# First keys in four pieces, weight inspections four to a slot, and token rows split behind a slot's values, in a two-layer gated cross-attention kernel

## The chip, the core and the metric

The kernel runs on one core of a Trainium2 chip. A core has five engines that run their own instruction queues in order and wait for each other by semaphores: TensorE (PE in the profile; its weight loads are PEld), VectorE (DVE), ScalarE (ACT), GpSimd (POOL), and SyncE (SP), which here only issues transfers. Work lies in SBUF (128 partitions) and matrix products are summed in PSUM, in banks of 128 x 512 f32. The metric is the device time of one execution in microseconds (us), the median of several runs.

## The reference

Eight images (B = 8) of 100 query tokens x of width 512 each attend to 722 context tokens of their own, twice, and after each attention there is a feed-forward stage on the 800 tokens. What is computed:

```
x = x + tanh(g_xattn[0]) * attention0(layernorm(x), ctx, ctx, mask)      # 16 heads of 32
x = x + tanh(g_ffn[0])   * ffn0(layernorm(x))
x = x + tanh(g_xattn[1]) * attention1(layernorm(x), ctx, ctx)            # with an output projection
x = x + tanh(g_ffn[1])   * ffn1(layernorm(x))

ffn0: h = silu(x W1 * s1) * (x W2 * s2);  h = gelu(h H1 * t1);  h = gelu(h H2 * t2);  y = h W3 * s3
      # 512 -> 2048 -> 2048 -> 2048 -> 512, weights of ffn0 are -1, 0 or 1, with a scale for each output
ffn1: the same gated form with weights and activations rounded to few levels first
```

The change lies in attention0: its keys, its slots, and what is done beside them for ffn0.

## The kernel before, in words

**Stages.** Attention 0 takes the first 590 us or so, ffn0 follows in two halves of 400 tokens, then attention 1 and ffn1. There is no planner: the order of every engine's instructions is written out by the program's own order, with generators that are advanced at fixed places (`next(...)`, `yield`). `take(us)` advances the generator in `state["fill"]`, the TensorE work that fills gaps, by about so many us.

**Start.** SyncE issues the loads in this order: key bias, key weights `wk` (1 MB), the first 384 context tokens of image 0 (`load_ctx(0, 0)`, 768 KB), value weights `wv`, the first four images' tokens x, query weights, the rest of the context, the other tokens, and small things. `projections` makes keys `kT` (`make`, L313 to 351): for each of four output chunks `oc`, four products over the input chunks `c` are summed in one bank of the pool `ps_p` (two banks), and ScalarE copies the sum out with the bias. Then the values of the same context tokens, L334 to 349. Queries follow (`queries`, L355), fed by normalised rows (`ln_turned`, L167): VectorE computes `ln_v`, GpSimd the root by a power (`ln_root`, L150), VectorE refines it (`ln_rstd`, L153 to 162) and scales rows (`ln_apply`, L165), TensorE turns them.

**Slots.** `attention` (L389) runs over 8 images b and 4 groups oc of four heads: 32 slots. In a slot TensorE makes the scores of a group in two halves (four banks of `ps_sc`), VectorE adds the mask, takes maxima and writes the rows `p` (L410), and ScalarE takes exponents (L427). Between the halves and behind them the next image's keys and values are made. Then `between(b, oc)` is called, and `settle` (L512) finishes the slot before: six times TensorE turns a block of `p` into one of the two banks of `ps_t` (L442), ScalarE or VectorE copies it out (L447, L445), and `values` (L450) sums the products with v in a free part of the fifth block's bank; VectorE copies that out (L461). At an image's end `finish` (L463) normalises, adds to x and takes the row statistics.

**Beside the slots.** `inspections` (L711) looks at ffn0's weights before they are used: 88 blocks of 128 x 1024 f32 are fetched by GpSimd's own transfers (two buffers), the low halves of the words are added up by GpSimd (L733, L734), and at the end VectorE takes the maximum (L737), TensorE turns it, and VectorE writes a verdict of 0 or 1. With 0 the products of ffn0 in a short format are exact and nothing more is run; otherwise the whole is computed again in full f32 (not the case with these inputs). `between0` advances the inspections three times a slot:

```
    def between0(b, oc):
        nonlocal entering
        for _ in range(3):
            next(inspected, None)
        ...
        if (b, oc) == (B - 2, KC - 1):
            later["wv"] = weights(a["L1_Wv"], [P, KC, D], "wv1")
            entering = normalised(0, HI_LO[0])
        if (b, oc) >= (B - 2, KC - 1):
            later["xs"] = next(entering)
```

`normalised` (L597) prepares the first 400 tokens for ffn0. Its first step, in slot 27 (b = 6, oc = 3), is the tokens' root, of which GpSimd does the power, and the first image's rows; each further step, in slots 28 to 31, turns one image's rows (L182) into a bank of `ps_t`, and `split` (L588) writes a high part `xa` by ScalarE (L590) and a low part `xc` by VectorE (L591), chunk by chunk; VectorE makes the next image's rows. ffn0's first product is ready to run behind slot 31. Its weight blocks are loaded through GpSimd's queue (`block`, L583).

Of the kernel before, what the change touches and what calls it, by code (L numbers as in the profile page):

```python
# [9 lines left out]
F32 = mybir.dt.float32  # L10
# [16 lines left out]
P = 128  # L27
# [28 lines left out]
def flow(tc: tile.TileContext, a: dict, out: bass.AP, verdict):  # L56
# [30 lines left out]
    def room(shape, name, dtype=F32):  # L87
        return wts.tile(shape, dtype, tag="w", name=name, bufs=3)
# [7 lines left out]
    def weights(src, shape, name):  # L96
        t = room(shape, name)
        nc.sync.dma_start(t, src)
        return t
# [89 lines left out]

    def load_ctx(i, part):  # L190
        k0, kn = PARTS[i // B][part]
        t = rooms["ctx"].tile([P, KC, PARTS[0][0][1]], F32, tag="ctxT", name=f"ctxT{i}_{part}")
        nc.sync.dma_start(t[:, :, :kn], a["ctxT"][i % B][:, :, k0 : k0 + kn])
        ctx_tiles[i, part] = t
# [74 lines left out]
    def projections(i, wk, wv, bk, more):  # L269
# [43 lines left out]
        def make():  # L313
            for part, (k0, kn) in enumerate(PARTS[layer]):
                cT = ctx_tiles.pop((i, part))
                for oc in range(KC):
                    ps = ps_p.tile([P, 512], F32, tag="ps", name="ps_k")
                    for c in range(KC):
                        nc.tensor.matmul(  # L319
                            ps[:, :kn],  # L320
                            wk[:, c, oc * P : (oc + 1) * P],
                            cT[:, c, :kn],
                            start=(c == 0),
                            stop=(c == KC - 1),
                        )
                        if c == KC - 1:
                            nc.scalar.activation(
                                kT[:, oc, k0 : k0 + kn],
                                ps[:, :kn],
                                AF.Identity,  # L330
                                bias=bk[:, oc : oc + 1],
                            )
                        yield kn * MM
                for kc, (r0, rn) in enumerate(KEYS[layer]):  # L334
# [53 lines left out]

    def attention(layer, kv, follow, qT, bias_of, between, wo, bv, bo, pick):  # L389

# [140 lines left out]
        for b in range(B):  # L531
# [11 lines left out]
            for oc in range(KC):  # L543
# [19 lines left out]
                if held is not None:  # L563
                    ending = settle()
                held = (b, oc, v, ps, oT, sums)

        def last():
# [143 lines left out]
    def inspections():  # L711
# [24 lines left out]
        worst = small.tile([P, 1], F32, tag="worst", name="worst")  # L736
        nc.vector.reduce_max(worst, seen, axis=AX.X)  # L737
        pt = ps_t.tile([P, 512], F32, tag="pst", name="ps_seen")
        nc.tensor.transpose(pt[:1, :P], worst, ident)
# [235 lines left out]
    bk = load("L0_bk", [P, KC], "bk0")  # L975
    wk = weights(a["L0_Wk"], [P, KC, D], "wk0")
    load_ctx(0, 0)
    wv = weights(a["L0_Wv"], [P, KC, D], "wv0")
# [74 lines left out]
    def between0(b, oc):  # L1053
        nonlocal entering
        for _ in range(3):
            next(inspected, None)
        if oc == 1 and b + 1 < B:
            state["spare"] = mask_bias(b + 1)
            next(state["spare"])
        if oc == 2:  # L1060
            for _ in state["spare"]:
                pass
        if (b, oc) == (B - 2, KC - 1):
            later["wv"] = weights(a["L1_Wv"], [P, KC, D], "wv1")
            entering = normalised(0, HI_LO[0])
        if (b, oc) >= (B - 2, KC - 1):
            later["xs"] = next(entering)

    ending = attention(0, kv, follow0, qT, lambda b: biases[b], between0, None, bv, None, None)
    for _ in inspected:  # L1070
# [16 lines left out]

    def nothing():
        pass
# [151 lines left out]
    def between1(b, oc):  # L1241
# [26 lines left out]
        lambda b: zero.to_broadcast([S, SK]),  # L1268
        between1,
        wo,  # L1270
        None,
# [107 lines left out]
```

## Time and profile before

| | |
|---|---|
| median of 3 runs | 1755.31 us (1752.71 to 1758.7) |
| the profiled execution's own time | 1753.82 us |
| its span, first to last instruction | 1751.6 us |
| TensorE busy | 1682.2 us (96%) |
| GpSimd busy | 574.1 us (33%) |
| first matmul starts | 8.53 us |
| GpSimd's inspections | 84 of 88 by 414 us, the last four from 506.6 to 522.5 us |
| tokens' root on GpSimd | 505.56 us |
| ffn0's first product | 591.66 us |

How to read the profile: a line of the timeline has the start and the length in us, the engine, the kernel's line, the operation, what it writes and reads, and how many instructions are merged (x4); in brackets stands how long the engine had been idle before it, and what ended that wait. A line of the table of waits has who waited for whom, the total in us, how often, and the longest. Queues of transfers are named after the engine that issues them (SPq, POOLq). Matmul lengths are modelled and overlap; the distance from one start to the next is the surer number.

### The profile page before, as it was taken

To read this page: it belongs to the slowest core of one execution; us is meant where nothing else is said; L and a number is where in the kernel's file an instruction comes from. 1 tells how busy PE (TensorE), PEld (TensorE's weight loads), DVE (VectorE), ACT (ScalarE), POOL (GpSimd) and SP (SyncE) were. 2 spreads that over 40 slices of the span, in tenths; PEclk is the share of its full clock that TensorE was granted. 3 is DMA by queue.
4 is the path that set the end of the run, shared out by engine and by line. 5 is a ranking of instruction groups with operands and counts; after the bars stand their busy time and mean duration, and the time that the engine had idled before them with its cause. 6 is when DMAs were issued, how large, how long until landed. Compare 5 with 4: busy or idle time off the path is not lost.

```text
span 1751.6 us, 30454 instructions
## 1 busy us (share of the span) xinstructions
PE 1682.2 (96%) x12459; PEld 1292.0 (74%) x12459; DVE 848.0 (48%) x2349; ACT 663.6 (38%) x1404; POOL 574.1 (33%) x542
## 2 busy tenths in 40 slices
PE   8999999999988999999999999989999999998887
PEld 4555555555554799999999999868888888885554
DVE  2445466455545430154462110455555576667755
ACT  1143434344334553322232111335445544544442
POOL 0699999993030000000000000133334333310110
PEclk9999999999999999999999999999999999999999
DMA  6345445452030388778685555420001001001000
GB/s 213 121 137 170 148 144 163 148 164 74 25 113 15 121 266 271 256 255 300 206 274 191 168 178 182 152 66 24 24 24 30 24 24 30 24 27 54 10 10 22
DMA packets 63802, 212.31 MB, mean 121 GB/s; under 512 B 7410, under 2 KB 30450, under 8 KB 51294
## 3 DMA queue, kind: packets, MB, share of 16 engines
q0 software_dynamic: 25344, 138.42, 23.8%
q1 hardware_dynamic: 38310, 71.86, 13.5%
q8 instruction: 99, 1.62, 0.4%
q14 instruction: 49, 0.40, 0.1%
HBM read 205.48 MB, written 4.78 MB: 120 GB/s over the span
## 4 chain that ended last, share of the span: by engine, by line
PE 62%; POOL 15%; DVE 8%; issue 8%; DMA 5%; ACT 2%; SPq 0%; DVEq 0%; POOLq 0%; ACTq 0%
PE ps_h L610 27%; POOL seen L734 9%; PE ps_v L259 7%; PE ps_k L259 5%; POOL part L733 4%; PE ps_pT L442 3%; PE sc L401 3%; DMA w_seen<-in_h_w 3%; PE ps_w L688 3%; PE ps_k L319 2%; PE ps_gu L885 2%; PE ps_pT L454 2%; PE ps_q L368 2%; PE ps_wo L497 2%; PE ps_v L339 2%
## 5 line engine op out<-in xcount | busy, mean ns | idle before, releaser
L610 PE MATMUL ps_h<-hi,h 128*128 128x400 f32 x1024 | 355.0, 347 | 0.0
L610 PE MATMUL ps_h<-lo,h 128*128 128x400 f32 x1024 | 354.7, 346 | 0.0
L442 PEld LDWEIGHTS ps_pT<-ident,p 100*128 100x128 f32 (+3 forms) x1536 | 163.4, 138 | 100.4 <-issue 47.3
L427 ACT ACTIVATE p<-p,negm 100x722 f32<-100x722 f32 x256 | 228.1, 894 | 10.8 <-DVE negm L424 10.6
L339 PE MATMUL ps_v<-wv,ctxT 128*128 128x512 f32 (+3 forms) x432 | 215.0, 608 | 0.0
L319 PE MATMUL ps_k<-ctxT,wk 128*128 128x384 f32 (+3 forms) x576 | 204.0, 482 | 8.5 <-DMA ctxT<-in_ctxT 8.5
L442 PE MATMUL ps_pT<-ident,p 100*128 100x100 f32 (+3 forms) x1536 | 196.9, 251 | 15.8 <-DVE pT L445 8.6
L734 POOL TENSOR_TENSOR seen<-seen,part 128x1024 int32<-128x1024 int32 x88 | 209.3, 2379 | 7.5
L591 DVE TENSOR_TENSOR lo<-g,hi 128x400 fp32r<-128x400 f32 x96 | 55.3, 576 | 311.2 <-ACT hi L590 311.2
L610 PEld LDWEIGHTS ps_h<-hi,h 128*128 128x128 f32 x1024 | 192.8, 188 | 0.6
L610 PEld LDWEIGHTS ps_h<-lo,h 128*128 128x128 f32 x1024 | 192.5, 188 | 0.6
L445 DVE COPY pT<-ps_pT 128x400 f32<-128x400 f32 (+1 forms) x180 | 102.5, 570 | 126.3 <-PE ps_pT L442 126.3
L410 DVE CUSTOM_DVE_ANT_0 p<-sc,mask 100x361 f32<-100x361 f32 x256 | 121.2, 530 | 62.7 <-PE sc L401 62.5
L447 ACT COPY pT<-ps_pT 128x400 f32<-128x400 f32 (+2 forms) x204 | 100.0, 492 | 136.1 <-PE ps_pT L442 135.9
L319 PEld LDWEIGHTS ps_k<-ctxT,wk 128*128 128x128 f32 x576 | 101.2, 192 | 67.1 <-issue 30.2
L585 POOL DMA_DIRECT2D h<-in_h_w x64 | 33.9, 529 | 354.7 <-PE ps_h L610 333.5
L663 ACT ACTIVATE g<-ps_h,h_s 128x400 f32<-128x400 f32 x64 | 38.1, 596 | 259.4 <-PE ps_h L610 259.4
L410 DVE CUSTOM_DVE_ANT_0 p<-sc,zero 100x361 f32<-100x361 f32 x256 | 121.7, 530 | 24.1 <-PE sc L401 23.6
L339 PEld LDWEIGHTS ps_v<-wv,ctxT 128*128 128x128 f32 (+3 forms) x432 | 69.5, 185 | 55.0 <-issue 53.4
L213 POOL TENSOR_SCALAR ctx_h<-ctx_raw 128x480 fp32r<-128x480 f32 (+1 forms) x40 | 23.8, 594 | 243.1 <-PE ps_v L259 196.1
L733 POOL CAST part<-w_seen 128x1024 int32<-128x1024 uint16 x88 | 92.7, 1053 | 21.6 <-DMA w_seen<-in_h_w 12.0
L259 PE MATMUL ps_k<-ctx_h,wk_g 128*128 128x240 f32 (+1 forms) x336 | 89.5, 293 | 2.9 <-DVE kT L294 1.7
(205 smaller groups left out, 2912.1 us busy)
## 6 DMA issues: line engine op xcount, KB each, us to landing
h<-in_h_w POOLq DMA_DIRECT2D x64, 1024.0 KB, 5.3
w_seen<-in_h_w POOLq DMA_DIRECT2D x64, 512.0 KB, 4.0
w<-in_w POOLq DMA_DIRECT2D x16, 1024.0 KB, 6.3
w_seen<-in_w POOLq DMA_DIRECT2D x16, 512.0 KB, 4.0
w_gate<-in_w_gate SPq DMA_DIRECT2D x16, 512.0 KB
w_up<-in_w_up SPq DMA_DIRECT2D x16, 512.0 KB
w_down<-in_w_down SPq DMA_DIRECT2D x16, 512.0 KB
w<-in_w_w POOLq DMA_DIRECT2D x8, 1024.0 KB, 7.0
```

What stands on the lines that cost most here:

```text
L259: nc.tensor.matmul(ps[:, col : col + n], w if keys_move else x, x if keys_move else w, start=(c == 0 and k == which[0]), stop=(c == KC - 1 ...
L319: nc.tensor.matmul(ps[:, :kn], wk[:, c, oc * P : (oc + 1) * P], cT[:, c, :kn], start=(c == 0), stop=(c == KC - 1),)
L339: nc.tensor.matmul(ps[:rn, :], cT[:, c, r0 - k0 : r0 - k0 + rn], wv[:, c, :], start=(c == 0), stop=(c == KC - 1),)
L410: nc.vector.tensor_tensor_reduce(ps[j][:, cols], sc[j][:S, :HALF], bias[:, cols], 1.0, LOWEST, ALU.add, ALU.max, m2[:, j, h : h + 1],)
L427: nc.scalar.activation(ps[j], ps[j], AF.Exp, bias=negm[:, j : j + 1], accum_out=sums[:, 4 * oc + j : 4 * oc + j + 1],)
L442: nc.tensor.transpose(pt[:kn, j, :], ps[j][:, k0 : k0 + kn], ident[:S, :S])
L445: nc.vector.tensor_copy(sb[:kn], pt[:kn])
L447: nc.scalar.copy(sb[:kn], pt[:kn])
L591: nc.vector.tensor_sub(two[1][:, cols], src, two[0][:, cols].bitcast(F32))
L610: nc.tensor.matmul(acc[:, :TH], w[:, c, :], part, start=(c == 0 and k == 0), stop=(c == len(ins) - 1 and k == len(two) - 1),)
L733: nc.gpsimd.tensor_copy(part, low)
L734: nc.gpsimd.tensor_tensor(seen, seen, part, ALU.add)
```

## The change

1. `load_ctx(0, 0)` and the load of `wk` become eight transfers: for each input chunk c, the chunk of `wk` and then the chunk of the context. For image 0's first part `make` runs its sixteen products with c outside and oc inside, in four banks of `ps_sc` at once. Everything else in `make` keeps its order.
2. `between0` advances the inspections four times a slot in slots 0 to 21 (88 steps), where it was three in slots 0 to 29.
3. The maximum over the inspection (a new `yield` stands behind it) is taken in slot 29, its transposition and the verdict in slot 30; both were in slot 29.
4. The steps of `normalised` move from `between0`, ahead of `settle`, into `beyond0`, which `attention` calls behind `settle`. Creating the generator and loading the second layer's value weights stay in `between0`. Attention 1 is given a `beyond` that does nothing.

```diff
--- before.py
+++ after.py
@@ -187,10 +187,15 @@
 
     ctx_tiles = {}
 
-    def load_ctx(i, part):
+    def load_ctx(i, part, beside=None):
         k0, kn = PARTS[i // B][part]
         t = rooms["ctx"].tile([P, KC, PARTS[0][0][1]], F32, tag="ctxT", name=f"ctxT{i}_{part}")
-        nc.sync.dma_start(t[:, :, :kn], a["ctxT"][i % B][:, :, k0 : k0 + kn])
+        if beside is None:
+            nc.sync.dma_start(t[:, :, :kn], a["ctxT"][i % B][:, :, k0 : k0 + kn])
+        else:
+            for c in range(KC):
+                nc.sync.dma_start(beside[0][:, c, :], beside[1][:, c, :])
+                nc.sync.dma_start(t[:, c, :kn], a["ctxT"][i % B][:, c, k0 : k0 + kn])
         ctx_tiles[i, part] = t
 
     def split_ctx(i, part, idle=False):
@@ -313,24 +318,32 @@
         def make():
             for part, (k0, kn) in enumerate(PARTS[layer]):
                 cT = ctx_tiles.pop((i, part))
-                for oc in range(KC):
-                    ps = ps_p.tile([P, 512], F32, tag="ps", name="ps_k")
-                    for c in range(KC):
-                        nc.tensor.matmul(
+
+                first = i == 0 and part == 0
+                home, tag = (ps_sc, "sc") if first else (ps_p, "ps")
+                order = [(oc, c) for oc in range(KC) for c in range(KC)]
+                if first:
+                    order.sort(key=lambda t: t[1])
+                sums = {}
+                for oc, c in order:
+                    if c == 0:
+                        sums[oc] = home.tile([P, 512], F32, tag=tag, name="ps_k")
+                    ps = sums[oc]
+                    nc.tensor.matmul(
+                        ps[:, :kn],
+                        wk[:, c, oc * P : (oc + 1) * P],
+                        cT[:, c, :kn],
+                        start=(c == 0),
+                        stop=(c == KC - 1),
+                    )
+                    if c == KC - 1:
+                        nc.scalar.activation(
+                            kT[:, oc, k0 : k0 + kn],
                             ps[:, :kn],
-                            wk[:, c, oc * P : (oc + 1) * P],
-                            cT[:, c, :kn],
-                            start=(c == 0),
-                            stop=(c == KC - 1),
+                            AF.Identity,
+                            bias=bk[:, oc : oc + 1],
                         )
-                        if c == KC - 1:
-                            nc.scalar.activation(
-                                kT[:, oc, k0 : k0 + kn],
-                                ps[:, :kn],
-                                AF.Identity,
-                                bias=bk[:, oc : oc + 1],
-                            )
-                        yield kn * MM
+                    yield kn * MM
                 for kc, (r0, rn) in enumerate(KEYS[layer]):
                     if not k0 <= r0 < k0 + kn:
                         continue
@@ -386,7 +399,7 @@
 
 
 
-    def attention(layer, kv, follow, qT, bias_of, between, wo, bv, bo, pick):
+    def attention(layer, kv, follow, qT, bias_of, between, beyond, wo, bv, bo, pick):
 
         gate = tg[:S, layer : layer + 1]
 
@@ -563,6 +576,7 @@
                 if held is not None:
                     ending = settle()
                 held = (b, oc, v, ps, oT, sums)
+                beyond(b, oc)
 
         def last():
             for _ in exps:
@@ -735,6 +749,7 @@
             yield
         worst = small.tile([P, 1], F32, tag="worst", name="worst")
         nc.vector.reduce_max(worst, seen, axis=AX.X)
+        yield
         pt = ps_t.tile([P, 512], F32, tag="pst", name="ps_seen")
         nc.tensor.transpose(pt[:1, :P], worst, ident)
         most = small.tile([1, 1], F32, tag="most", name="most")
@@ -973,8 +988,8 @@
     rooms["oT"] = pool(right, "oT0", 2, side="right")
 
     bk = load("L0_bk", [P, KC], "bk0")
-    wk = weights(a["L0_Wk"], [P, KC, D], "wk0")
-    load_ctx(0, 0)
+    wk = room([P, KC, D], "wk0")
+    load_ctx(0, 0, (wk, a["L0_Wk"]))
     wv = weights(a["L0_Wv"], [P, KC, D], "wv0")
     x = const.tile([S, B, D], F32, tag="x", name="x")
     nc.sync.dma_start(x[:, :BH], a["x"][:, :BH])
@@ -1052,7 +1067,10 @@
 
     def between0(b, oc):
         nonlocal entering
-        for _ in range(3):
+
+        for _ in range(4 if 4 * (b * KC + oc) < 2 * (HC // 2 + 2 * HC + HC // KC) else 0):
+            next(inspected, None)
+        if (b, oc) in ((B - 1, KC - 3), (B - 1, KC - 2)):
             next(inspected, None)
         if oc == 1 and b + 1 < B:
             state["spare"] = mask_bias(b + 1)
@@ -1063,10 +1081,12 @@
         if (b, oc) == (B - 2, KC - 1):
             later["wv"] = weights(a["L1_Wv"], [P, KC, D], "wv1")
             entering = normalised(0, HI_LO[0])
+
+    def beyond0(b, oc):
         if (b, oc) >= (B - 2, KC - 1):
             later["xs"] = next(entering)
 
-    ending = attention(0, kv, follow0, qT, lambda b: biases[b], between0, None, bv, None, None)
+    ending = attention(0, kv, follow0, qT, lambda b: biases[b], between0, beyond0, None, bv, None, None)
     for _ in inspected:
         pass
     for _ in state["fill"]:
@@ -1085,7 +1105,7 @@
     def home_2(oc):
         return homes[2, 0]
 
-    def nothing():
+    def nothing(*_):
         pass
 
     def second_tokens():
@@ -1267,6 +1287,7 @@
         second["qT"],
         lambda b: zero.to_broadcast([S, SK]),
         between1,
+        nothing,
         wo,
         None,
         bo,
```

## The prediction

> **What bounds the kernel now.** I read the page first. TensorE is busy for 96% of the span, so a gain must come from the rest, or from matmuls that run slowly.
>
> ```profile
> span 1751.6 us, 30454 instructions
> PE 1682.2 (96%) x12459; PEld 1292.0 (74%) x12459; DVE 848.0 (48%) x2349; ACT 663.6 (38%) x1404; POOL 574.1 (33%) x542
> ```
>
> Then the waits of TensorE over the whole span, to see what the 69 us are made of.
>
> ```profile
> PE ps_pT L442 <- DVE pT L445: 8.6, 11, 4.5
> PE ps_k L319 <- DMA ctxT<-in_ctxT: 8.5, 1, 8.5
> PE ps_pT L442 <- DVE xc L591: 4.9, 4, 1.4
> ...
> PE ps_seen L739 <- DVE worst L737: 1.8, 1, 1.8
> ```
>
> Columns: total us, times, longest. The change touches four of them: the first wait for data (8.5), the longest single wait for a copied probability block (4.5, of the 8.6), the four waits for the tokens' split (4.9), and the wait for the inspection's maximum (1.8). The third view is the timeline where the 4.5 lies, slot 27 (image 6, last head group; slots are counted over image and head group, 32 in all).
>
> ```profile
> 411.25 2.70 POOL L734 TENSOR_TENSOR seen<-seen,part 128x1024 int32<-128x1024 int32 x1
> 505.56 1.03 POOL L150 TENSOR_TENSOR ln_r<-ln_v,root 100x4 f32<-100x4 f32 x1 [91.61 <-DVE ln_v L144]
> 506.57 0.59 POOL L724 DMA_DIRECT2D w_seen<-in_w_w  x1
> ```
> ```profile
> 506.63 1.61 DVE L157 TENSOR_TENSOR ln_u<-ln_r 100x4 f32<-100x4 f32 x1 [1.15 <-POOL ln_r L150]
> 508.47 2.20 DVE L159 TENSOR_SCALAR ln_u<-ln_u 100x4 f32<-100x4 f32 x1
> 510.90 1.58 DVE L165 TENSOR_SCALAR xn<-x,mv,ln_rstd 100x512 f32<-100x512 f32 x1
> 513.35 0.93 PE L442 MATMUL ps_pT<-ident,p 100*128 100x100 f32 x4 [4.50 <-DVE pT L445]
> ```
>
> GpSimd does its inspections as fast as it can, not at the slots' pace: it has finished 84 by 414 us and then stands 91.6 us before the tokens' root, which is queued ahead of the last four. When the root is done at 506.6, those four start, and VectorE's small steps beside them take 1.61, 2.20 and 1.58 us. The same three took 0.16, 0.17 and 0.54 at 21 us, where GpSimd was idle. VectorE's copies are queued behind; TensorE waits 4.5 us. The last view is the granted clock.
>
> ```profile
> 414.00:500.00 86.00, 86.00 (x675) 49.23 (x674) 43.52 (x139) 38.75 (x86) 0.00 (x0) 1.00 0.13 42
> 505.00:513.40 8.40, 3.90 (x20) 1.89 (x18) 6.97 (x11) 1.05 (x3) 7.66 (x7) 0.96 0.35 107
> 513.40:521.20 7.80, 7.80 (x73) 4.36 (x73) 1.83 (x4) 3.93 (x10) 7.17 (x6) 0.61 0.30 88
> ```
>
> After the length come PE, PEld, DVE, ACT and POOL busy, then the granted clock: TensorE loses no time from 414 to 500, and after the 4.5 us wait runs at 0.61 for 7.8 us.
>
> **Part 1: the first keys in pieces.** Two transfers (weights 1.049 MB, context 0.786 MB) become eight, and the sixteen products of the first part go by input chunk, not by output chunk. Bytes moved, from windows of half and whole microseconds, add up to 0.47 MB at 4.0 us and 1.84 MB at 7.5; the first matmul starts at 8.53, 1.05 later. The first pair of pieces is 0.459 MB, reached at 3.98; with the same 1.05 the start is 5.0, a gain of 3.5. Bounds: a 2 KB load issued at 0.73 lands at 2.46, 1.73 later, so a piece issued until about 2.3 lands at 4.1 at best (gain 4.4); at worst the first matmul still waits for the last piece (a rival below). I take 3.5, from the rows of these very transfers.
>
> The later pieces are hidden: eight issues by the 0.42 to 0.66 us of SP's rows end by 6.5 and the bytes arrive by about 8.5, while the fourth chunk is wanted at about 15.5. That follows from the clock: the first eight matmul instructions take until the eviction at 14.03, the next three groups 2.82, 2.58, 2.58; the first eight thus cost 2.9 us more than the rest (5.7 us at half rate), and 24 take 10.5. SP's later issues move by up to 4 us: the value weights, x, the query weights. SP's rows show each load waiting for the one eight before it (gates for wv, then x, then wq); with six more, wv waits for the first piece and x for the second, both landed by 5. The transfers behind are limited by bytes, so x should land near its 16.38; its first rows are ready at 22.4 and wanted at 31.25 less 3.5, a cover of 5.3 us, and each us beyond it would show. Four banks of the scores' pool hold the sums; no score needs them before 65 us. The four evictions by ScalarE (0.58 each) now come together, beside 9 us of values.
>
> The Trainium skill (TensorE: Matmul & The Clock Gate, Part 1: The HAM clock gate) says that the array starts at half rate and is released by a free-running window of some 3.4 us that must be busy. By that an estimated 3.4 to 6.8 us would be slow, against the 5.7 read here, and the whole sum below would be 14.9 or 13.2 instead of 13.7.
>
> **Part 2: four inspections in a slot.** 88 steps now end in program order with slot 21, ahead of the root. GpSimd needs about 4.3 us a step (84 from 54 to 414), so the last four run until some 430 less 3.5, and the root at about 500 finds it idle: 70 us of cover. No GpSimd time is saved, only the neighbourhood. The price of slot 27: from its first transposes to the next scores 505.04 to 520.38, 15.34 us; the same stretch of slot 23, with the same number of value products, is 443.20 to 450.87, 7.67. Gain 7.7, the 4.5 of waiting and 3.2 of slow matmuls. Lower end 6.0: the root's chain, now behind the values, is 2.7 us of VectorE (ln_v 0.2, 1.15 until the root, four small steps 0.8, rows 0.54) ahead of the next reductions. They would end at 5.1 us after the values instead of 2.8; the second half of the scores is wanted from 4.7 to 5.3 and takes the banks one by one as they come free, so I charge nothing. The four steps now beside slots 22 and 23: TensorE waited 3.8 us for blocks in 350 us of inspection, so 0.2 for 16 us. On GpSimd's queue the first w12 load moves up from 522.5; it needs the old value weights' buffer and is wanted only at 591, as before.
>
> **Part 3: the maximum a slot ahead of its transposition.** The reduction (1.21 us on VectorE) stays in slot 29, its transposition moves to slot 30: TensorE's 1.8 us wait goes. VectorE, already late there from an image's ending (it ends its last reduction at 546.2, 3 us after the scores), still carries 1.2 us ahead of the block copies. Followed through with the rows' durations, the fourth transposition waits 0.75 us for the second copy; bounds 0 and 1.8.
>
> **Part 4: tokens split behind the values.** In slots 28 to 31 TensorE waited 1.36, 1.07, 1.37 and 1.12 us since the rows' turning held one of two banks while ScalarE and VectorE alternated four times (0.57 a pair). Those 4.9 us go. What is late next: the turning now takes the bank in which the values were summed, so it waits for their copy: values end at 538.3, copy L461 runs 538.48 to 538.74, a new wait of 0.5 in each of four slots, 2.0. Behind it ScalarE and VectorE alternate until 3.3 us after the values; reductions run to 5.2, against scores wanted from 5.3 on: nothing, with little to spare. ScalarE's third and fourth exponents slip from 0.7 to 5.1, wanted at 8. In slot 31 the feed-forward's first product stands directly behind: it waits 0.5 for the first split chunk, and then three times 0.2 since a pair takes 0.57 and two products 0.36: 1.1.
>
> **Sum.** Gains 3.5 + 7.7 + 1.8 + 4.9 = 17.9; costs 0.2 + 0.75 + 2.0 + 1.1 = 4.05, say 4.2 with the shorter covers: 13.7 us. The feed-forward behind is bound by TensorE (27.85 of 28 us from 592) and everything in it is issued relative to it, so nothing gives the gain back. The profiled execution took 1753.82 us (span 1751.6), 0.1% under the median of three, 1755.31: 1753.8 - 13.7 = 1740.
>
> **Rivals.** (B) The alternation after the values is exposed: VectorE has so little to spare that each of slots 28 to 31 loses 1.5 us and slot 28 another 1.7 to the root's chain. For: 5.2 against 5.3. Against: VectorE is idle 2.7 us ahead of the second reductions in slots 28 and 30. Gain 13.7 - 7.7 = 6.0, 1748. (C) The pieces do not do what they are for: the first matmul waits for whole tiles, with the last piece at 8.5 to 9.5. Against: x is also loaded in two transfers, and its first statistics ran at 16.38 without the second half, 6.3 MB into the queue. Gain 13.7 - 4.2 = 9.5, 1744. (D) Slower: the wait of slot 27 moves to the slots' ends. If TensorE waits 4.5 us behind the values, the clock falls as at 513 us, 7.7 us a time; with three of the five slots 27 to 31 so, 23.1 - 13.7 = 9.4 us are lost, 1763; with two, 15.4, the kernel is back at 1755.5. It decides where the chain after the values is over 4.5 us longer than the cover; I find at most 2.7 of it and the clock held at 1.00 through waits of 1.8. (E) The inspections beside slots 22 and 23 stop VectorE for a whole step each time: 4 x 2.36 = 9.4, gain 4.3, 1749.5. For: the 2.20 us row. Against: three visible waits in the 84 steps before.
> The Trainium skill (SBUF — State Buffer, Who interferes with whom) has this as a rule: GpSimd and VectorE share a port pair, and whichever comes second is blocked for the whole instruction. The 1.61 and 2.20 us rows agree, while most of the 84 earlier steps cost TensorE nothing.
>
> **How the numbers follow.** Chances: forecast 0.64 (own range 1735 to 1746: start 2.5 to 4.4, slot 27 from 6.0, slot 29 from 0 to 1.8, clock a us either way, and the runs' own spread of 3 us), B 0.14, C 0.09, D 0.07, E 0.04, and 0.02 for a start at 4.1 with all covers holding, 1737. 0.3%, 5.3 us, is about what can be told from no change. Faster: 0.64 + 0.09 + 0.02 + half of B = 0.82; same: E and half of B, 0.11; slower: D, 0.07. The range 1733 to 1749 leaves out D, E, and a tenth at the edges of the rest.
>
> **What would show it.** Right: first ps_k near 5.0; GpSimd's last inspection near 427 and an idle GpSimd beside the small ln steps, at 0.16 to 0.2 each; no wait for pT over 1 us and clock 1.00 in slot 27; no wait for xc ahead of ps_pT, and 0.5 us waits of ps_xn for the copy L461. Wrong: a first ps_k after 8 us (C); waits of the scores on the reductions in slots 28 to 31 (B); a clock under 1 there (D); new pT waits near 425 (E).

## The result, and the profile after

The changed kernel takes 1744.61 us (median of four runs, 1742.39 to 1745.94) against 1755.42 us for the kernel before beside it (four runs, 1752.71 to 1758.7). The ratio is 0.993, with a 95% interval of 0.9914 to 0.9947: it is faster by 12.3 us by the ratio (9.3 to 15.1), or 10.8 by the two medians. The profiled execution of the changed kernel took 1745.94 us, with a span of 1743.8; it is the slowest of its four.

The page of the changed kernel; the last line is its chain, the share of the span by engine.

```profile
span 1743.8 us, 30463 instructions
PE 1683.4 (97%) x12459; PEld 1292.1 (74%) x12459; DVE 848.3 (49%) x2349; ACT 663.7 (38%) x1404; POOL 573.6 (33%) x542
...
PE 85%; DVE 11%; ACT 2%; DMA 1%; issue 1%; POOL 0%; SPq 0%; DVEq 0%; ACTq 0%
```

TensorE has as much to do as before, in 7.8 us less, and GpSimd has left the chain; the same line of the kernel before was

```profile
PE 62%; POOL 15%; DVE 8%; issue 8%; DMA 5%; ACT 2%; SPq 0%; DVEq 0%; POOLq 0%; ACTq 0%
```

The waits of TensorE over the span:

```profile
PE ps_pT L467 <- DVE pT L458: 6.1, 5, 1.6
PE ps_k L332 <- DMA ctxT<-in_ctxT: 6.0, 1, 6.0
...
PE ps_pT L455 <- DVE pT L458: 4.9, 11, 0.7
```

The first data come at 6.0 instead of 8.5, no block copy by VectorE is waited for longer than 0.7 us ahead of a transposition, and the waits for `xc` and for `worst` are gone. But the top line has grown: products with the values that wait for a block's copy, up to 1.6 us at a time. Before the change it was

```profile
PE ps_pT L454 <- DVE pT L445: 4.0, 4, 1.3
```

The timeline of the tokens' root in the changed kernel:

```profile
428.42 2.36 POOL L748 TENSOR_TENSOR seen<-seen,part 128x1024 int32<-128x1024 int32 x1
...
516.27 1.03 POOL L150 TENSOR_TENSOR ln_r<-ln_v,root 100x4 f32<-100x4 f32 x1 [85.49 <-DVE ln_v L144]
517.34 0.16 DVE L157 TENSOR_TENSOR ln_u<-ln_r 100x4 f32<-100x4 f32 x1 [1.15 <-POOL ln_r L150]
517.73 0.17 DVE L159 TENSOR_SCALAR ln_u<-ln_u 100x4 f32<-100x4 f32 x1
518.13 0.55 DVE L165 TENSOR_SCALAR xn<-x,mv,ln_rstd 100x512 f32<-100x512 f32 x1
```

The last inspection ends at 430.8, and VectorE's steps take 0.16, 0.17 and 0.55 us again. The same windows of the clock as before the change (length, then busy PE, PEld, DVE, ACT, POOL, the granted clock, the transfers):

```profile
505.00:513.40 8.40, 8.40 (x43) 4.19 (x42) 3.60 (x13) 2.50 (x6) 0.00 (x0) 1.00 0.17 63
513.40:521.20 7.80, 7.80 (x82) 4.39 (x80) 4.30 (x18) 4.07 (x9) 1.59 (x2) 1.00 0.35 111
```

Where the time went is best seen slot by slot. In the table, stretch n runs from the start of the value products of slot n-1 (lines L454 and L467, on TensorE) to those of slot n. A slot is finished within the next one, so stretch 26 lies where the prediction says slot 27. The four columns on the right are experiments told below. All are differences of starts in the timelines, in us.

| | before | after | four steps + maximum only | tokens' split only | maximum late | before, light | after, light |
|---|---|---|---|---|---|---|---|
| values of slot 0 start | 100.55 | 97.70 | 99.20 | 99.80 | 98.01 | 99.51 | 97.16 |
| stretches 1 to 25 | 396.28 | 402.07 | 395.68 | 397.80 | 396.89 | 390.93 | 390.93 |
| 26 | 22.12 | 14.71 | 14.92 | 14.70 | 14.70 | 21.93 | 14.71 |
| 27 | 18.15 | 16.20 | 17.90 | 23.22 | 16.21 | 17.89 | 16.20 |
| 28 | 19.11 | 16.05 | 19.87 | 20.64 | 20.63 | 19.10 | 16.05 |
| 29 | 17.84 | 16.51 | 18.15 | 16.41 | 16.41 | 17.85 | 16.52 |
| 30 | 16.44 | 15.25 | 16.43 | 15.25 | 15.25 | 16.44 | 15.25 |
| 31 | 12.21 | 14.04 | 12.19 | 14.04 | 14.03 | 12.21 | 14.02 |
| rest of the span | 1148.9 | 1151.3 | 1151.6 | 1148.2 | 1151.1 | 1148.2 | 1151.4 |

Between the two profiled executions, the start gives 2.85 us and stretches 26 to 31 give 13.1 (7.41 + 1.95 + 3.06 + 1.33 + 1.19 - 1.83). Stretches 1 to 25, in which the change adds no work to TensorE, take 5.8 back, and the rest of the span 2.4: 7.8 in all.

What happens in stretches 1 to 25 shows in the changed kernel's timeline of slot 17, where image 5's mask is made:

```profile
352.47 2.35 POOL L748 TENSOR_TENSOR seen<-seen,part 128x1024 int32<-128x1024 int32 x1
352.66 2.56 DVE L1027 CAST mask<-mask 100x722 f32<-100x722 int32 x1
...
356.47 2.35 POOL L748 TENSOR_TENSOR seen<-seen,part 128x1024 int32<-128x1024 int32 x1
356.55 2.68 DVE L1032 TENSOR_SCALAR mask<-mask,mask_m 100x722 f32<-100x722 f32 x1
...
359.15 0.56 DVE L458 COPY pT<-ps_pT 82x400 f32<-82x400 f32 x1
359.76 0.38 PE L467 MATMUL ps_pT<-pT,v 82*32 82x100 f32 x8 [1.57 <-DVE pT L458]
```

```profile
362.00:363.00 1.00, 1.00 (x4) 0.54 (x3) 0.86 (x4) 0.21 (x2) 1.00 (x2) 0.50 0.75 299
363.00:364.00 1.00, 1.00 (x3) 0.61 (x2) 0.00 (x0) 0.00 (x0) 0.45 (x2) 0.50 0.11 45
364.00:365.00 1.00, 1.00 (x4) 0.61 (x3) 0.00 (x0) 0.00 (x0) 0.92 (x2) 0.67 0.77 217
```

Each mask step begins just behind an addition of GpSimd and ends 0.4 us after it. The sixth block's copy stands behind the second one on VectorE, TensorE waits 1.57 us for it, and soon after runs at half clock for some 3.4 us. Stretch 17 is 18.80 us long, against 15.38 before the change. The same wait of 1.57 us stands at 232.04 and at 296.15 us, and there the clock stayed at 1.00. Of the 5.8 us, 4.0 lie in stretches 5, 9, 13 and 17, where masks are made, and 1.8 in stretch 8, behind the end of an image.

### The profile page after: what moved, and what is told of

It is laid out like the page before. It is cut to its first block, busy times and chain, and to the rows that moved or that the text cites. A ratio compares the mean times of both kernels' runs of the same rounds, so it can differ in the third digit from the quotient of the medians.

```text
span 1743.8 us, 30463 instructions
## 1 busy us (share of the span) xinstructions
PE 1683.4 (97%) x12459; PEld 1292.1 (74%) x12459; DVE 848.3 (49%) x2349; ACT 663.7 (38%) x1404; POOL 573.6 (33%) x542
## 4 chain that ended last, share of the span: by engine, by line
PE 85%; DVE 11%; ACT 2%; DMA 1%; issue 1%; POOL 0%; SPq 0%; DVEq 0%; ACTq 0%
PE ps_h L624 27%; PE ps_k L332 10%; PE ps_v L352 8%; PE ps_v L264 7%; PE ps_pT L455 6%; PE sc L414 6%; PE ps_k L264 5%; PE ps_pT L467 4%; PE ps_w L702 3%; PE ps_q L381 3%; PE ps_gu L900 2%; PE ps_wo L510 2%; DVE p L423 1%; PE ps_down L954 1%; DVE pT L458 1%; DVE st L137 1%
## 5 line engine op out<-in xcount | busy, mean ns | idle before, releaser
L440 ACT ACTIVATE p<-p,negm 100x722 f32<-100x722 f32 x256 | 228.2, 894 | 12.2 <-DVE negm L437 12.1
L264 PE MATMUL ps_v<-wv_g,ctx_h 128*120 128x256 f32 (+1 forms) x336 | 90.9, 295 | 0.5 <-DVE v L313 0.5
```

What stands on the lines that cost most here:

```text
L264: nc.tensor.matmul(ps[:, col : col + n], w if keys_move else x, x if keys_move else w, start=(c == 0 and k == which[0]), stop=(c == KC - 1 ...
L440: nc.scalar.activation(ps[j], ps[j], AF.Exp, bias=negm[:, j : j + 1], accum_out=sums[:, 4 * oc + j : 4 * oc + j + 1],)
```

## The experiments

Two explanations of the missing microseconds stood against each other. One: VectorE's mask steps meet GpSimd's additions, and the change moves more of them together. The other: the changed parts themselves are worth less than their waits, because what was late moves on to the next place. The parts were run alone first.

**Part 1 alone.** The kernel before, with the first keys in pieces and nothing else.

```diff
     bk = load("L0_bk", [P, KC], "bk0")
-    wk = weights(a["L0_Wk"], [P, KC, D], "wk0")
-    load_ctx(0, 0)
+    wk = room([P, KC, D], "wk0")
+    load_ctx(0, 0, (wk, a["L0_Wk"]))
```

The edits of `load_ctx` and `make` are those of the change.

> Part 1 alone: keys in pieces, inspections three to a slot, split ahead of settle. In the changed kernel the values of slot 0 start 2.85 us earlier, and between slot 8 and slot 20 5.7 us are lost. My theory: the loss comes from VectorE's mask steps meeting GpSimd's additions at another phase, because the slots moved by 2.8 us against GpSimd's 4 us steps; then this kernel has it too: 2.85 us ahead at slot 0, 2 to 6 us lost in slots 8 to 20, the 22.1 us slot 26 to 27 unchanged, 1753 to 1758 us. Rival one, four inspections to a slot cause the loss: 2.85 us kept throughout, 1752.5. Rival two, the loss is chance of one execution: anything between, and not repeated in the same slots.

Measured: 1752.88 us (nine runs) against 1756.32, ratio 0.9988 (0.9973 to 1.0004). The first product starts at 5.3 us, but the values of slot 0 start only 2.49 us earlier, and stretches 8, 9 and 17 take 17.84, 18.85 and 17.11 us, against 16.10, 16.85 and 15.38 before, while 13 takes 15.36 against 16.77: by slot 25 the kernel is 1.57 us behind. Its waits of TensorE between 20 and 30 us have one line more:

```profile
PE ps_v L352 <- ACT v L361: 1.7, 1, 1.7
```

So the lead is real, part of it goes at once into a wait of the first values, and in this execution the slots ate the rest, by work that this edit did not touch. Over the nine runs that is not shown: their median lies 3.4 us under that of the kernel before, about the whole lead, with an interval that takes in no gain at all.

**Parts 2 and 3 alone**, with the split of the tokens left ahead of `settle`.

```diff
-        for _ in range(3):
+        for _ in range(4 if 4 * (b * KC + oc) < 2 * (HC // 2 + 2 * HC + HC // KC) else 0):
+            next(inspected, None)
+        if (b, oc) in ((B - 1, KC - 3), (B - 1, KC - 2)):
             next(inspected, None)
```

The new `yield` behind the maximum, as in the change, is in it too.

> Parts 2 and 3 alone: whole loads at the start, four inspections to a slot, maximum in slot 29 and its transposition in slot 30, split still ahead of settle. Theory: GpSimd is idle beside the root's chain, so VectorE's small steps take 0.2 us again and the 4.5 us wait and the slow clock of slot 27 go, but 2.7 us of VectorE still stand ahead of the copies: 1 us of wait; the wait of 1.8 for the maximum goes and the four waits for the split (4.9) stay. Slots 8 to 20 as before, for the phase is that of before: 1755.4 - 6.7 - 1.8 = 1747. Rival, four to a slot causes the loss in slots 8 to 20: 1752.

Measured: 1752.32 us (twelve runs), ratio 0.9984 (0.9971 to 0.9997), 5 us above the theory; the profiled execution, at 1748.06, is the fastest of the twelve. In it slots 8 to 20 cost no more than before, so that its rival, 1752, has the number and not the cause. Stretch 26 falls from 22.12 to 14.92: the root's chain may well stand ahead of the block copies, if GpSimd is idle beside it. But stretch 28 grows from 19.11 to 19.87, although the wait for the maximum is gone. The waits of TensorE in it, 527.7 to 547.6 us, are one line:

```profile
PE ps_pT L455 <- DVE xc L605: 2.4, 1, 2.4
```

Before, the same stretch had 1.8 for `worst` and 1.1 for `xc`, 2.9 in all. The maximum's 1.21 us still stand on VectorE ahead of the split, and the split is what TensorE waits for, in one piece. So the waits shrank by half a microsecond; what makes the stretch longer is the clock behind the wait:

```profile
540.80:544.20 3.40, 3.40 (x11) 1.83 (x9) 0.57 (x1) 1.73 (x4) 0.00 (x0) 0.50 0.00 0
```

Half clock for 3.4 us costs about 1.7 (an estimate, 3.4 at half rate); without it the stretch would be some 0.9 shorter than before, not 0.8 longer. In this execution part 3 without part 4 gained nothing.

**Part 4 alone**, with three inspections in a slot.

```diff
         if (b, oc) == (B - 2, KC - 1):
             later["wv"] = weights(a["L1_Wv"], [P, KC, D], "wv1")
             entering = normalised(0, HI_LO[0])
+
+    def beyond0(b, oc):
         if (b, oc) >= (B - 2, KC - 1):
             later["xs"] = next(entering)
```

> Part 4 alone: split behind the values, inspections three to a slot, so that the last four steps of GpSimd start right behind the root. Theory: the chain of 7 us on VectorE (1.6, 2.2 and 1.6 in it) now stands ahead of the reductions of slot 28, whose cover is about 3.8 us: the second half of the scores waits about 3 us instead of 4.5 plus 3.2 of slow clock; the 4.9 us of split waits go, 1.8 are lost at the feed-forward's start, 1.8 for the maximum stay: 1755.4 - 4.7 - 4.9 + 1.8 = 1747.6. Rival, moving the split is all that matters and the neighbours on GpSimd nothing: 1755.4 - 7.7 - 4.9 + 1.8 = 1744.6.

Measured: 1753.85 us (twelve runs), ratio 0.999 (0.9976 to 1.0005), above both the theory and the rival. Stretch 26 is 14.70, but 27 is 23.22. Its timeline:

```profile
516.83 2.35 POOL L748 TENSOR_TENSOR seen<-seen,part 128x1024 int32<-128x1024 int32 x1
...
517.00 2.20 DVE L159 TENSOR_SCALAR ln_u<-ln_u 100x4 f32<-100x4 f32 x1
...
519.44 1.58 DVE L165 TENSOR_SCALAR xn<-x,mv,ln_rstd 100x512 f32<-100x512 f32 x1
...
521.52 2.88 PE L414 MATMUL sc<-kT,xb 32*100 32x361 f32 x8 [3.34 <-DVE m L423]
```

The chain of slow steps has moved behind the values, with GpSimd still at work beside it; the reductions come late, and the next scores wait 3.34 us. From 520 to 524 us the clock is 0.65, from 524 to 528 it is 0.50. This is rival D, at its place and near its price: 7.0 us over the 16.20 of stretch 27 in the changed kernel. It needs a busy GpSimd; part 2 is what removes it.

**Without the meetings.** To price GpSimd's neighbourhood, its two steps of an inspection were cut to one column: in the changed kernel in all 88, in the kernel before in the first 84 (the last four, beside the root, were left whole).

```diff
-            nc.gpsimd.tensor_copy(part, low)
-            nc.gpsimd.tensor_tensor(seen, seen, part, ALU.add)
+            nc.gpsimd.tensor_copy(part[:, :1], low[:, :1])
+            nc.gpsimd.tensor_tensor(seen[:, :1], seen[:, :1], part[:, :1], ALU.add)
```

> The changed kernel with GpSimd's conversions and additions of the inspection cut to one column each, so the verdict is drawn from one column in 1024; its transfers stay as they are. Theory (the loss in slots 8 to 20 is VectorE's mask steps behind GpSimd's additions): no wait for copied blocks between slot 0 and slot 25, the 2.85 us kept, 1744.6 - 5.8 = 1739. Rival, the loss comes from the transfers or from chance: the waits stay in number, 1743 to 1745.

> The kernel before with GpSimd's conversions and additions of the first 84 inspection steps cut to one column each (the verdict is drawn from the last four blocks and one column of the others); the last four stay whole. What the additions cost the kernel before in slots 0 to 25, to be set against the 11.1 us that they cost the changed one. Theory A, the change made these meetings dearer: before loses about 5.4 us (its profiled slots 5, 9, 13 and 16): 1756.3 - 5.5 = 1751. Theory B, both lose the same on the mean and the profiled execution of before was a lucky one: 1756.3 - 11 = 1745. In both the 22.1 us of slot 26 to 27 stay.

Measured: 1733.52 us (four runs) for the changed kernel, ratio 0.9866 (0.9847 to 0.9885); 1748.7 us (six runs) for the kernel before, ratio 0.9962 (0.9949 to 0.9974). In both, stretches 1 to 25 take 390.93 us, within a hundredth: there, nothing else makes the two kernels differ. The neighbourhood costs the kernel before 7.6 us (1756.3 - 1748.7) and the changed one 11.1 (1744.6 - 1733.5). The kernel before lies between its theories A and B, at 1751 and 1745. The difference of the two, 3.5, is uncertain by about 5 us (an estimate from the intervals of the three ratios): that meetings cost both kernels is shown, that the change made them dearer is likely and not shown. Without the neighbourhood, the change is worth 15.2 us (1748.7 - 1733.5), and at slot 31 the two executions are 15.0 apart: 2.35 from the start, 7.22 from stretch 26, 5.45 from 27 to 31. Groups of VectorE in the changed kernel, then in its light form (busy us, mean ns of one):

```profile
L1027 DVE CAST mask<-mask 100x722 f32<-100x722 int32 x8 | 14.8, 1852 | 0.0
L1032 DVE TENSOR_SCALAR mask<-mask,mask_m 100x722 f32<-100x722 f32 x8 | 14.4, 1805 | 0.3
L494 DVE TENSOR_TENSOR t<-t,brow 100x512 f32<-100x512 f32 x8 | 8.5, 1066 | 0.3
L1030 DVE TENSOR_REDUCE mask_m<-mask 100x1 f32<-100x722 f32 x8 | 7.1, 892 | 0.0
```

```profile
L1030 DVE TENSOR_REDUCE mask_m<-mask 100x1 f32<-100x722 f32 x8 | 7.2, 896 | 0.0
L494 DVE TENSOR_TENSOR t<-t,brow 100x512 f32<-100x512 f32 x8 | 5.5, 692 | 0.3
L1032 DVE TENSOR_SCALAR mask<-mask,mask_m 100x722 f32<-100x722 f32 x8 | 4.8, 598 | 0.3
L1027 DVE CAST mask<-mask 100x722 f32<-100x722 int32 x8 | 4.2, 527 | 0.0
```

The conversion, the scaling and the addition of two rows pay; the reduction, between the same neighbours, pays nothing. The Trainium skill (SBUF — State Buffer, Who interferes with whom) names just these: a cast, a scaling by a scalar, or an operation with two inputs in SBUF can block against GpSimd, a reduction on trn2 never does. The groups above agree in all four.

**The mask off VectorE's contested forms.** If that is the cause, it can be removed without touching GpSimd: VectorE takes the maximum straight from the integers and scales that one column, and ScalarE converts and scales the mask in one step.

```diff
-        nc.vector.tensor_copy(mf, mi)
-        yield
...
-        nc.vector.reduce_max(mm, mf, axis=AX.X)
+        nc.vector.reduce_max(mm, mi, axis=AX.X)
+        yield
+        nc.vector.tensor_scalar_mul(mm, mm, -MASK_C)
...
-        nc.vector.tensor_scalar(mf, mf, mm, MASK_C, ALU.subtract, ALU.mult)
+        nc.scalar.activation(mf, mi, AF.Identity, scale=MASK_C, bias=mm)
```

On the changed kernel:

> The changed kernel with the mask's two large steps taken from VectorE: its maximum is read from the integers by VectorE, and one ScalarE instruction scales and shifts it. Theory (the mask's conversion and scaling wait out GpSimd's additions, 2.6 us in place of some 0.8): the losses of the second slot of an image (8.5 us in slots 5, 9, 13 and 17 of the profile) go, ScalarE's 0.9 us costs at most 0.3 a slot: 1744.6 - 7 = 1737.5. Rival (it is the endings of an image, with their sums of two SBUF operands, or the copies themselves): 1743 to 1745, the second slots stay at 16.8 to 18.8.

On the kernel before:

> The kernel before with the mask's two large steps taken from VectorE, as it was done to the changed one. Theory: before loses 4.4 us to these two steps in its profile, the change moved the slots to where they meet more often; so this version gains about 5 (1751), less than the 9.4 that the changed kernel gained, and the change is then worth 16 us on top (1751 - 1735). Rival: both gain the same 9.4 (1747), and the meetings are not dearer in the changed kernel.

Measured: the changed kernel with it takes 1735.16 us (four runs), ratio to the kernel before 0.9879 (0.9863 to 0.9895), which beats both kernels. The kernel before with it takes 1749.46 (twelve runs), ratio 0.9967 (0.9954 to 0.9981). So it is worth 9.4 us in the one (1744.6 - 1735.2) and 6.0 in the other (1755.5 - 1749.5), which again lies between theory (5) and rival (9.4), and the change on top of it 14.3. In both, stretches 5, 9, 13 and 17, where the masks are made, are down to 15.33 or 15.34 us. What is left lies in stretches 8, 12 and 20 (17.18, 16.66 and 17.19 with the change), behind the endings of images. The rows in stretch 8 of the changed kernel with the mask on ScalarE:

```profile
213.54 2.34 POOL L748 TENSOR_TENSOR seen<-seen,part 128x1024 int32<-128x1024 int32 x1
213.58 2.84 DVE L494 TENSOR_TENSOR t<-t,brow 100x512 f32<-100x512 f32 x1
```

Alone this step takes 0.69 us. It, too, was met by an addition; so is the update of x behind it (L517), which takes 0.75 us alone and 2.72 at 277.67 us of the same execution.

**The start.** Two orders of the first transfers, one execution each: the tokens x ahead of the value weights, and the context's pieces issued by ScalarE, the weights' by SyncE.

```diff
-    wv = weights(a["L0_Wv"], [P, KC, D], "wv0")
     x = const.tile([S, B, D], F32, tag="x", name="x")
     nc.sync.dma_start(x[:, :BH], a["x"][:, :BH])
+    wv = weights(a["L0_Wv"], [P, KC, D], "wv0")
```
```diff
-                nc.sync.dma_start(t[:, c, :kn], a["ctxT"][i % B][:, c, k0 : k0 + kn])
+                nc.scalar.dma_start(t[:, c, :kn], a["ctxT"][i % B][:, c, k0 : k0 + kn])
```

> The changed kernel with the first images' x loaded ahead of the value weights. Theory (x came 2.5 us later, 18.9, and its rows on VectorE stood ahead of the copies of v): x lands near 12, TensorE's 0.5 us wait for v goes, values of slot 0 start at 97.1 instead of 97.7. Rival: the value weights come too late, TensorE waits for them at 18.2.

> The changed kernel with the four context pieces issued by ScalarE's queue, the weight pieces by SyncE's. If the first pair is late (6.02 instead of the forecast 5.0) since a single queue issues and feeds piece by piece, the first matmul starts near 5.2. If the rows of 1.5 and 2 KB themselves move slowly (200 to 330 GB/s until 5 us, where the kernel before had 400), it stays at 5.8 to 6.2.

Measured: 1744.98 and 1742.32 us, one execution each, the second 0.07 us below the fastest run of the changed kernel, so no difference in time is shown. With x first, its rows begin at 15.95 us and the first values no longer wait for their copy; they wait 0.68 for their weights instead, and slot 0's values start at 97.12. With two queues the first product starts at 5.87:

```profile
5.87 2.90 PE L332 MATMUL ps_k<-ctxT,wk 128*128 128x384 f32 x4 [5.87 <-DMA wk<-in_L_Wk]
```

That is inside the 5.3 to 6.0 of the others. So a second issuing queue did not bring the first piece sooner. What is left is how fast the pieces move; that it is the cause, and why they are slower, no run tested.

**The maximum where it was**, with everything else changed.

```diff
         worst = small.tile([P, 1], F32, tag="worst", name="worst")
         nc.vector.reduce_max(worst, seen, axis=AX.X)
-        yield
```

> The changed kernel with the maximum, its transposition and the verdict in one step in slot 29 again. Part 3 by itself, with the split behind the values: by the forecast the wait of 1.8 us for the maximum comes back and the stretch of slot 28 to 29 is 17.8 instead of 16.05. Rival: with the split gone from there, VectorE is free sooner and the wait is under 1 us, 16.8.

Measured: 1745.35 us, one execution. Stretch 28 takes 20.63 instead of 16.05:

```profile
536.84 1.21 DVE L751 TENSOR_REDUCE worst<-seen 128x1 f32<-128x1024 int32 x1
538.10 0.27 PE L753 MATMUL ps_seen<-ident,worst 128*1 128x128 f32 x1 [3.00 <-DVE worst L751]
```

The wait is 3.0 us and no longer 1.8, since nothing else holds TensorE back before it, and behind it the clock drops (0.74 and 0.69 in the two windows of 3 us from 537 on). Part 3 is worth 4.5 us over stretches 27 to 30 once part 4 stands (68.50 against 64.01), some 1.7 of it this fall of the clock.

This execution tells a second thing. Up to slot 25 it is the very same program as the changed kernel, yet its stretches 1 to 25 take 396.89 us where the profiled one took 402.07. Which mask steps and which sums at an image's end meet an addition differs from execution to execution. Over the light 390.93, the five executions that start early and have the mask on VectorE (the changed kernel, part 1 alone, the two of the start, this one) lost 11.1, 9.4, 8.6, 9.2 and 6.0 us; the three that start late (the kernel before, parts 2 and 3, part 4) lost 5.4, 4.8 and 6.9.

## Why the prediction was right, and where it was not

The measured 1744.61 us lies within the forecast range of 1733 to 1749 and on the forecast side of no change; the gain was 10.8 to 12.3 us instead of 13.7. Each of the four gains came, by the mechanism named for it. That the sum came so near is in part luck: stretches 27 to 30 gained 3.6 us more than was counted, and the slots ahead of them lost 3.5 to 5.8 that the sum did not have.

**The start, 3.5.** The first product moved by nearly that: it starts at 5.3 to 6.0 us in the executions with pieces (5.6 on average) and at 8.5 to 9.5 without (8.9), 3.3 earlier. Of the step's own figure of 5.0 the transfers fell short: from 2 to 5 us they moved some 0.59 MB, where the whole tiles had moved 0.87. Only part of the lead arrives: the values of slot 0 start 2.85 us earlier in the two profiled executions, 2.2 on average over the five of each kind that have the same order of loads. What went missing is in the cover of "5.3 us" for x. It was reckoned against the queries that want the rows; but VectorE's rows stand ahead of the copies of the first values in its queue, x came at 18.93 instead of 16.38, and the first values waited 0.5 to 1.7 us. The timeline of the changed kernel:

```profile
6.02 12.37 PE L332 MATMUL ps_k<-ctxT,wk 128*128 128x384 f32 x32 [6.02 <-DMA ctxT<-in_ctxT]
18.93 0.69 DVE L137 BATCH_NORM_STATS2 st<-x 100x6 f32<-100x512 f32 x1 [17.22 <-DMA x<-in_x]
25.72 2.84 PE L352 MATMUL ps_v<-wv,ctxT 128*128 128x512 f32 x6 [0.47 <-ACT v L361]
```

The slow stretch at the start was shorter by about a microsecond: the keys take 12.2 us until the values' first product, 1.9 over four groups of 2.58, where they had taken 2.9 over. The change did not do that: over the twelve profiled executions the keys take 12.0 to 13.0 us with pieces and 12.0 to 13.3 without. The prediction's sum by the Trainium skill (TensorE: Matmul & The Clock Gate, Part 1: The HAM clock gate) was 14.9 or 13.2 for a slow stretch of 3.4 or 6.8; at half rate the 1.7 to 3.0 us over of the twelve executions are stretches of 3.3 to 5.9, so they agree, with 3.8 in the changed kernel.

**Slot 27, 7.7.** Measured 7.41 in the pair and 7.22 between the light kernels. The reason given, the neighbourhood and not GpSimd's time, is shown by parts 2 and 3 alone, where the chain stays ahead of the copies and stretch 26 is 14.92 all the same.

**The maximum and the split, 6.7 of gains less 0.75 and 2.0.** Stretches 27 to 30 gained 7.5 instead of 3.95. Both costs failed to come. The turning was to wait 0.5 us in each slot for the copy L474 (L461 before) out of the same bank; it does not:

```profile
531.85 0.56 PE L182 MATMUL ps_xn<-ident,xn 100*128 100x100 f32 x4
532.06 0.26 DVE L474 COPY oT<-ps_pT 128x100 f32<-128x100 f32 x1 [1.58 <-PE ps_pT L467]
```

The turning starts before the copy of the sums. Whether it went past the copy in the same bank or had the other bank stays open: the trace shows no banks. And TensorE waits for nothing at all in stretch 28. One turning, about 0.4 us, is no gain, since it has only moved from stretches 27 to 30 into stretch 31. The two gains cannot be added up part by part, either. Over stretches 27 to 30 the maximum without the split lost 0.8 us (72.35 against 71.54), the split without the maximum, beside an idle GpSimd, gained 3.0 (68.50), and both together gained 7.5 (64.01). In each of the first two executions a fall of the clock for 3.4 us, about 1.7, is in the figure; without it they would be a gain of 0.9 and one of 4.7, together still under 7.5.

**ffn0's start, 1.1.** Stretch 31 is 1.83 longer. Of this 0.57 is the last image's turning (579.66 us), which stood in stretch 30 before. The wait was 0.33 instead of 0.5, and the products come at VectorE's and ScalarE's pace of 0.57 us a chunk for four pairs, where the step let three wait 0.2 each: some 1.26 in all, near the 1.1.

**"So 0.2 for 16 us".** This is the step that failed. It was read from waits that TensorE had shown, averaged over 350 us, and it priced four inspections moved beside slots 22 and 23; those cost 0.2 in the profiled execution (stretches 20 and 21 are 16.23 and 15.37 against 16.10 and 15.33) and 1.7 in the one with the late maximum (16.99 in stretch 21). What costs is the same meeting in all the slots before, 7.6 us before the change and 11.1 after by the medians: 3.5 where 0.2 stood, with the uncertainty told above, and 5.8 in the profiled pair. The prediction had the fact before it, as rival E, and put it aside because most of the 84 steps cost TensorE nothing. Most do not; but a mask step or a sum at an image's end does if it falls on an addition, and a lead of 3 us moves TensorE and VectorE against GpSimd, which goes at its own pace of about 4 us a step. Part 1 alone moved the meetings, and lost 9.4 in the slots of its one profiled execution; which of them are hit is not set by the program, and five executions are few to say by how much, or whether, an early start makes it worse.

**"The clock held at 1.00 through waits of 1.8".** It did where the prediction looked; in slot 17 of the changed kernel a wait of 1.57 was followed by 0.50, at two other places of the same execution it was not.

**The rivals.** B did not come: no score waits for a reduction in slots 28 to 31, and stretch 28 has no wait at all. C is excluded by the 6.0 us of the first product. D came only with part 4 alone. E, as it was priced for the four moved steps, did not come in the profiled execution (0.2 us); its mechanism is what costs the slots before them.

**"Nothing gives the gain back" behind ffn0's start.** The rest of the span took 2.4 us more in the pair. Over all twelve profiled executions it lies between 1148.2 and 1153.7. What differs is the clock: half of the time at half clock taken off, what is left varies by 2.4 us over the twelve and no longer by 5.5. The traces also show why such falls come in some executions and not in others. In each trace the stretches of half clock start a whole number of 3.413 us apart, so the clock is set on a fixed beat. Over all traces, from 30 to 1720 us, a step of this beat at full clock that matmul rows, by their modelled lengths, filled to less than 0.46 was followed by half clock in every one of 42 cases, one filled to more than 0.68 in none; in between both came. So it matters how a wait lies in the beat: the wait that ends at 232.04 us of the changed kernel is cut in two by it. It does not settle every case, as two steps of the same execution show, the first followed by half clock, the second not:

```profile
357.80:361.20 3.40, 1.83 (x37) 0.89 (x26) 2.74 (x5) 1.13 (x3) 3.31 (x4) 1.00 0.84 231
292.94:296.35 3.41, 1.84 (x50) 1.00 (x48) 3.40 (x3) 0.00 (x0) 3.41 (x3) 1.00 0.73 217
```

What decides between them stays open.

## What to carry to other kernels

Where GpSimd runs long element-wise steps at its own pace, list VectorE's conversions, scalings and two-input operations that can fall beside them, and price each at the length of GpSimd's step: their mean against their shortest time shows it at a glance. Move those to ScalarE or to a reduction before tuning the order around them; any edit that shifts the start will otherwise change which of them are hit, and hide a gain of several microseconds. Test parts that share a queue together as well as apart, and look at the clock before a part is called worthless: here one part lost 0.8 us alone and another gained 3.0, each with about 1.7 lost to the clock, and together they gained 7.5.

## What the runs showed of the hardware

- A VectorE conversion of 100x722 took 0.53 us alone and 2.56 beside an addition on GpSimd that began 0.19 before it; the scaling took 0.60 and 2.68, the addition of two rows 0.69 and 2.84. They end 0.4 to 0.5 us after the addition, sooner than their whole length alone, which fits standing still until it ends and not being slowed all along. GpSimd's conversion, 1.05 us long, did the same to a lesser extent: the mask's conversion beside one took 1.39 (418.92 us of the changed kernel). Reductions of the mask took 0.89 to 0.91 in either case.
- A wait of 1.57 us was followed by half clock for 3.4 us at one of three places of the changed kernel (it ended at 359.76 us; not where it ended at 232.04 and 296.15). The Trainium skill (TensorE: Matmul & The Clock Gate, Why this matters for your kernels) advises against gaps over some 3 us between matmul bursts; here half of that was enough at one place, and the measurement decides.
- Stretches of half clock start a whole number of 3.413 us apart in each trace.
- Eight transfers of one chunk each moved 0.59 MB from 2 to 5 us where two whole ones had moved 0.87 (over all twelve executions 0.58 to 0.71 and 0.78 to 0.91), and a second issuing queue did not bring the first product forward (5.87 us).
